# Expert blocks of a decoder layer: where results wait before their scatter, when the sums are loaded, and how the last group is summed

## The chip, the cores and the metric

The kernel runs on one core of a Trainium2 chip. The metric is device time in microseconds; lower is better. A core has a matrix engine (PE; its weight loads are listed as PEld), a vector engine (DVE), a scalar engine (ACT), a general engine (POOL) that also issues the scatters by row number, and a queue engine (SP) that issues most other transfers. The 16 DMA engines carry all transfers. Each engine works through its own list of instructions in order.

## The reference

The input is 32 sequences of 128 rows with 128 features, and a context of the same shape. One decoder layer is computed: causal self-attention with 16 heads, a residual and a layernorm; cross-attention to the context, a residual and a layernorm; then a mixture of eight experts of which each row uses two, a residual and a layernorm.

```python
def _moe(x, rw, rb, w1, b1, w2, b2):
    router_weights = softmax(xf @ rw + rb)
    topw, topi = top_k(router_weights, 2)
    topw = softmax(topw)
    h = gelu(einsum('td,edf->etf', xf, w1) + b1)     # D = 128, FF = 512, E = 8
    eo = einsum('etf,efd->etd', h, w2) + b2
    out = einsum('etd,te->td', eo, combine)
x = layernorm(x + attn(x, x, x, ..., causal))
x = layernorm(x + attn(x, ctx, ctx, ...))
x = layernorm(x + moe(x, ...))
```

All is in float32.

## The kernel before

The 32 sequences form eight groups of four. Attention is a schedule of half slots: `half_slot(h)` does half of the scores of one sequence, parts of older ones, and then the calls that a table holds for that half slot (projections, norms, routing, row scatters). The table is filled by `chain` and `book`, which put each step into the half slot that is least booked by estimated costs.

The experts work on blocks of 128 rows. Each row of x2, the result after the second layernorm, is scattered to two rows of a DRAM buffer `xs` in the order of the experts (L789). There are two phases of four groups each, each with its own buffers and 39 blocks, so 78 blocks in all, 32 row scatters of the second phase and 78 result scatters. The first phase's blocks start once its rows are placed; the routing and the row scatters of the second phase's last groups run beside them, one half slot after each block.

A block needs its expert's weights (`wd`, 514 KB, five places, so four blocks ahead; L854 or L858 on SP), its rows (`xt`, four blocks in one load, L841) turned by PE (`px`, L870) and copied by DVE (`xT`, L885), the first layer (L893), the gelu on ACT (L898), the second layer (L909), a copy of the result by DVE (`ot`, L914), and a scatter of its 128 rows by POOL to the DRAM buffer `eo` (L916). `ot` has four places: the copy of block i waits until the scatter of block i-4 has landed. PE, DVE, ACT, POOL and SP each take the blocks in the order in which `Pipeline.run` writes them: weights of block i+4, first layer of i, second layer and scatter of i-1, and then `beside`, which holds a half slot of attention's end and one step of each running sum.

The sums: when enough result scatters of a group have been issued (`needed(g)` plus four blocks, planned in `summed`), `combine` loads the residual (`acc`, L982) and the group's results (`gt`, L984, which waits on SP until those scatters have landed), waits four steps, adds the two weighted results (L1001), and normalizes (`finish`, `normalize`: statistics on DVE, a power on POOL at L342, four scalings on ACT at L347, two products with the norm's gain and bias on DVE at L1010 and L1012), then stores (L1014). After the last block the sums that are left run alone.

## Time and profile before

The median of three runs is 653.02 us (649.6 to 657.02).

| | |
|---|---|
| profiled execution, its own time | 657.72 us |
| its span on the core | 655.9 us |
| mean granted TensorE clock | 0.953 |
| PE busy | 583.9 us (89%) |
| DVE busy | 434.5 us (66%) |
| ACT busy | 379.8 us (58%) |
| POOL busy | 368.8 us (56%) |
| moved by DMA over the span | 82.52 MB, 126 GB/s on average |

The shares of busy time are averages over attention and experts, which differ: attention needs little of the DMA engines, the blocks need much of them. A stretch must be read by itself. The chain of waits is followed back from the last instruction; a group of instructions is named by its line, engine, and the tiles it writes and reads. A matmul's end is modelled, so a busy PE is not always one at its peak.

### The profile page before, as it was taken

How to read it: one execution, taken by the hardware profiler on the slowest of the kernel's cores; microseconds unless marked ns; L12 is line 12 of the kernel's file. 1: busy time of each engine (PE TensorE's matmuls, PEld its weight loads, DVE VectorE, ACT ScalarE, POOL GpSimd, SP SyncE). 2: the span in 40 equal slices, each digit the busy share in tenths (PEclk: the TensorE clock that was granted, in tenths of full speed). 3: DMA queues.
4: the chain of work that ended last, by engine and by line, in shares of the span. 5: the costliest groups of instructions: out<-in, count | busy, mean ns of one | idle time of the engine just before them, and what ended most of it. 6: DMA issues, size and time to landing. Idle time of an engine off the chain costs nothing.

```text
span 655.9 us, 22713 instructions
## 1 busy us (share of the span) xinstructions
PE 583.9 (89%) x9247; PEld 496.1 (76%) x9247; DVE 434.5 (66%) x1359; ACT 379.8 (58%) x855; POOL 368.8 (56%) x749
## 2 busy tenths in 40 slices
PE   8999899999999799999999988997898888998970
PEld 6777677887877578877777776776887788898970
DVE  4356556767758867887788778984966644543553
ACT  3255456677676357666666666555674456664652
POOL 3256455544645456628836614743888885654661
PEclk9599979999999899999999998997998989999995
DMA  5114420614010011001001100421887999999962
GB/s 138 27 32 71 96 36 2 213 33 168 3 34 3 1 37 49 3 2 55 14 19 31 39 2 10 151 96 49 278 271 230 356 343 370 362 348 389 345 249 74
DMA packets 48040, 82.52 MB, mean 126 GB/s; under 512 B 7968, under 2 KB 26464, under 8 KB 47936
## 3 DMA queue, kind: packets, MB, share of 16 engines
q1 hardware_dynamic: 42816, 71.57, 33.7%
q0 software_dynamic: 4544, 9.38, 3.9%
q8 instruction: 72, 1.18, 0.8%
q14 instruction: 32, 0.26, 0.1%
q10 hardware_dynamic: 576, 0.13, 0.1%
HBM read 62.15 MB, written 23.10 MB: 130 GB/s over the span
## 4 chain that ended last, share of the span: by engine, by line
PE 62%; DVE 20%; DMA 8%; ACT 4%; issue 3%; POOL 3%; SPq 0%; ACTq 0%; DVEq 0%; POOLq 0%
PE ph L893 8%; PE po L909 7%; PE sc_s L453 6%; PE sc_c L453 6%; PE po_s L539 4%; DMA wd<-wpk 4%; DVE m_c L492 4%; PE st_s L465 4%; PE po_c L539 4%; PE sc_s L447 3%; DVE m_s L492 3%; DMA eo<-ot,to 2%; PE st_s L460 2%; PE st_c L460 2%; PE pk_s L396 1%
## 5 line engine op out<-in xcount | busy, mean ns | idle before, releaser
L898 ACT ACTIVATE h<-ph,wd 128x128 f32<-128x128 f32 x312 | 89.0, 370 | 64.1 <-PE ph L893 28.4
L504 POOL TENSOR_SCALAR_AFFINE_SELECT pr_s<-pr_s 128x1024 f32<-128x1024 f32 x64 | 70.1, 1096 | 82.6 <-ACT pr_s L500 82.2
L492 DVE TENSOR_REDUCE m_s<-sc_s 128x8 f32<-128x1024 f32 x64 | 78.2, 1222 | 55.2 <-PE sc_s L453 53.9
L916 POOL DMA_INDIRECT eo<-ot,to x78 | 77.8, 998 | 52.2 <-DVE acc L1001 12.5
L500 ACT ACTIVATE pr_c<-st_c 128x1024 f32<-128x1024 f32 x64 | 65.5, 1024 | 63.2 <-PE st_c L465 61.0
L500 ACT ACTIVATE pr_s<-st_s 128x1024 f32<-128x1024 f32 x64 | 65.5, 1024 | 57.4 <-PE st_s L465 57.2
L893 PE MATMUL ph<-xT,wd 128*128 128x128 f32 x624 | 87.8, 285 | 12.3 <-DMA wd<-wpk 5.5
L492 DVE TENSOR_REDUCE m_c<-sc_c 128x8 f32<-128x1024 f32 x64 | 78.0, 1218 | 24.3 <-PE sc_c L453 16.6
L893 PEld LDWEIGHTS ph<-xT,wd 128*128 128x128 f32 x624 | 78.6, 198 | 17.8 <-DMA wd<-wpk 5.7
L909 PE MATMUL po<-wd,h 128*128 128x128 f32 x624 | 84.2, 279 | 2.2 <-ACT h L898 2.2
L453 PE MATMUL sc_c<-k_c,qb_c 32*128 32x128 f32 x1024 | 75.2, 285 | 11.0 <-DVE m_c L492 9.3
L909 PEld LDWEIGHTS po<-wd,h 128*128 128x128 f32 x624 | 77.5, 195 | 2.8 <-ACT h L898 2.8
L453 PE MATMUL sc_s<-k_s,qb_s 32*128 32x128 f32 x1024 | 76.3, 290 | 0.0
L453 PEld LDWEIGHTS sc_c<-k_c,qb_c 32*128 32x128 f32 x1024 | 62.9, 188 | 17.4 <-DVE m_c L492 13.0
L465 PE MATMUL st_s<-qb_s,k_s 32*128 32x128 f32 x1024 | 72.5, 281 | 0.0
L789 POOL DMA_INDIRECT xs<-x,slots x64 | 64.1, 1002 | 13.0 <-issue 12.4
L465 PE MATMUL st_c<-qb_c,k_c 32*128 32x128 f32 x1024 | 70.5, 276 | 0.0
L465 PEld LDWEIGHTS st_s<-qb_s,k_s 32*128 32x128 f32 x1024 | 67.4, 192 | 0.9
L453 PEld LDWEIGHTS sc_s<-k_s,qb_s 32*128 32x128 f32 x1024 | 67.2, 199 | 0.1
L465 PEld LDWEIGHTS st_c<-qb_c,k_c 32*128 32x128 f32 x1024 | 65.9, 188 | 0.2
L914 DVE COPY ot<-po 128x128 f32<-128x128 f32 x78 | 22.5, 290 | 62.3 <-PE po L909 53.3
L447 PE MATMUL sc_s<-causal,quarter 32*128 32x512 bf16 (+3 forms) x512 | 48.5, 309 | 9.0 <-DVE m_s L492 8.5
(249 smaller groups left out, 1203.6 us busy)
## 6 DMA issues: line engine op xcount, KB each, us to landing
wd<-wpk SPq DMA_DIRECT2D x78, 514.0 KB
xs<-blank SPq DMA_DIRECT2D x2, 2600.0 KB
xt<-xs SPq DMA_DIRECT2D x20, 260.0 KB
wpk<-in_L_xattn_e_w_dram SPq DMA_DIRECT2D x16, 256.0 KB
gt<-eo SPq DMA_DIRECT2D x8, 512.0 KB
xg<-in_x_dram SPq DMA_DIRECT2D x8, 256.0 KB
eg<-in_ctx_dram SPq DMA_DIRECT2D x8, 256.0 KB
x2d<-base SPq DMA_DIRECT2D x8, 256.0 KB
```

What stands on the lines that cost most here:

```text
L447: nc.tensor.matmul(sc[:, i, :, k], lhsT=quarter[rowsof(g), j, :], rhs=bc(causal[rowsof(g), j, k], 1, 4), start=j == 0, stop=False,)
L453: nc.tensor.matmul(sc[:, i, r, :], lhsT=new.group.qb[rowsof(g), r, new.b, :], rhs=new.group.k[rowsof(g), new.b, :], start=not new.masked, ...
L465: nc.tensor.matmul(st[:, i, r, :], lhsT=old.group.k[rowsof(g), old.b, :], rhs=old.group.qb[rowsof(g), r, old.b, :], start=False, stop=r == 3,)
L492: nc.vector.tensor_reduce(new.m[:, 8 * half : 8 * half + 8], sc.rearrange("p i r k -> p (i r) k"), AX.X, ALU.max,)
L500: nc.scalar.activation(old.pr[:, hs, :], st.rearrange("p i r k -> p (i r) k"), AF.Exp, scale=SCALE)
L504: nc.gpsimd.affine_select(out=old.pr[:, hs, :], in_=old.pr[:, hs, :], pattern=[[0, 8], [1, P]], compare_op=ALU.is_ge, fill=0.0, base=0, ch ...
L539: nc.tensor.matmul(po[VC * r : VC * r + VC, g, :], lhsT=u.group.v[:, u.b, at_v : at_v + VC], rhs=u.pr[:, h, :], start=e == 0, stop=e == 1,)
L789: i = nc.gpsimd.indirect_dma_start(out=xs[ph.p][:, :], out_offset=bass.IndirectOffsetOnAxis(ap=slots[:, k, t : t + 1], axis=0), in_=gr.x2[ ...
L893: nc.tensor.matmul(hid[:, c, :], lhsT=w[:, c * P : (c + 1) * P], rhs=self.xT[i // XB][:, i % XB, :], start=True, stop=True,)
L898: nc.scalar.activation(self.h[i][:, c, :], hid[:, c, :], AF.Gelu, bias=w[:, B1 + c : B1 + c + 1])
L909: nc.tensor.matmul(po, lhsT=h[:, c, :], rhs=w[:, W2 + c * P : W2 + (c + 1) * P], start=c == 0, stop=c == NFC - 1,)
L916: s = nc.gpsimd.indirect_dma_start(out=eo[p][:, :], out_offset=bass.IndirectOffsetOnAxis(ap=self.to[q][:, i % XB : i % XB + 1], axis=0), i ...
```

## The change

Results of four blocks share a tile, and there are eleven such tiles, taken in turn from places that attention used (four of `k`, four of `x1`, three of `xT0`). The scatter is a step of its own, `send`: after each block, up to 1.6 scatters a block are issued, less the row scatters that the half slot issued, oldest result first. The target row numbers `to` get ten places instead of three. A sum begins when six more scatters than it needs have been issued (two more for the group before the last), `acc` gets three places, and one more step lies before the store. The x2 of the last two groups is made by DVE instead of POOL. The first rows are fetched and turned a few half slots earlier. The last group is summed in two pairs with operations of their own, and stored by SP and ACT in two transfers.

```diff
+SCATTERS = 1.6
+HELD = ("k",) * 4 + ("x1",) * 4 + ("xT0",) * 3
...
-        nc.gpsimd.tensor_tensor(x2, gr.y, bc(lng[1], 1, G), ALU.mult)
+        engine = nc.vector if gr.gi >= NG - 2 else nc.gpsimd
+        engine.tensor_tensor(x2, gr.y, bc(lng[1], 1, G), ALU.mult)
         yield
-        nc.gpsimd.tensor_tensor(x2, x2, bc(lnb[1], 1, G), ALU.add)
+        engine.tensor_tensor(x2, x2, bc(lnb[1], 1, G), ALU.add)
...
-            self.to[q] = moe.tile([P, XB], U32, tag="to", name=f"to_{p}_{q}", bufs=3)
+            self.to[q] = moe.tile([P, XB], U32, tag="to", name=f"to_{p}_{q}", bufs=10)
...
-            ot = moe.tile([P, P], F32, tag="ot", name=f"ot_{p}_{i}", bufs=4)
-            nc.vector.tensor_copy(ot, po)
+            if q not in self.ot:
+                n = Blocks.held = (Blocks.held + 1) % len(HELD)
+                self.ot[q] = (io if HELD[n] == "xg" else act).tile(
+                    [P, XB, P], F32, tag=HELD[n], name=f"ot_{p}_{q}", bufs=HELD.count(HELD[n])
+                )
+            nc.vector.tensor_copy(self.ot[q][:, i % XB, :], po)
+
+        def send(self, i):
+            q, p = i // XB, self.ph.p
             nc.gpsimd.memset(apart, 0.0)
             s = nc.gpsimd.indirect_dma_start(
...
-                in_=ot, in_offset=None,
+                in_=self.ot[q][:, i % XB, :], in_offset=None,
...
+        def send(self, others):
+            self.may = min(self.may + SCATTERS - others, 2.0)
+            while self.may >= 1.0 and self.ready:
+                k, i = self.ready.pop(0)
+                k.send(i)
+                self.may -= 1.0
...
                 if before:
                     before[0].second_layer(before[1])
+                    self.ready.append(before)
...
+    def last_sums(gr, gt):
+        rs = [small.tile([P, 2, 2], F32, tag="rs", name=f"rs_l{ab.start}") for ab in PAIRS]
+        for n, ab in enumerate(PAIRS):
...
+            for b in range(2):
+                y, t = gr.acc[:, ab.start + b, :], G * gr.gi + ab.start + b
+                for k in range(2):
+                    nc.vector.scalar_tensor_tensor(
+                        y, gt[:, ab.start + b, P * k : P * k + P], wts[:, k, t : t + 1], y,
+                        ALU.mult, ALU.add,
+                    )
+                nc.vector.bn_stats(st[:, b, :], y)
...
+            (nc.sync, nc.scalar)[n].dma_start(
+                out=out[G * gr.gi + ab.start : G * gr.gi + ab.stop].rearrange("b p d -> p b d"),
+                in_=y,
+            )
...
-        gr.acc = moe.tile([P, G, P], F32, tag="acc", name=f"acc_{gr.gi}")
+        gr.acc = moe.tile([P, G, P], F32, tag="acc", name=f"acc_{gr.gi}", bufs=3)
...
-        for _ in range(4):
+        if gr.gi == NG - 1:
+            yield
+            last_sums(gr, gt)
+            return
+        for _ in range(3 if gr.gi == NG - 2 else 4):
             yield
...
-    at(start - 1, blocks.first_rows)
+    at(start - 5, blocks.first_rows)
+    at(start - 2, blocks.turn)
...
-                i = needed(g) + 4
-                key = (p, i) if i < NBL[p] or p == NP - 1 else (p + 1, i - NBL[p])
-                summed[key] = groups["c", g0 + g]
+        def begin_sums():
+            while unsummed:
+                p, g = unsummed[0]
+                if len(phases[p].done) < min(needed(g) + (2 if p == NP - 1 and g == n_last - 2 else 6), NBL[p]):
+                    break
+                sums.append(combine(groups["c", PHASES[p][0] + g]))
+                unsummed.pop(0)
...
         def beside(ph, i):
+            rows = sum(len(phase.sent) for phase in phases)
...
+            blocks.send(sum(len(phase.sent) for phase in phases) - rows)
+            begin_sums()
             step()
+            if ph.p == NP - 1 and i >= NBL[-1] - 3:
+                step()
...
-        sums.extend(combine(gr) for _, gr in sorted(summed.items()))
+        begin_sums()
+        last = sums.pop()
+        next(last)
+        while sums:
+            step()
+        sums.append(last)
         while sums:
             step()
```

## Prediction

> **What bounds the kernel now.** I read the busy time by stretches first, cut where the work changes: expert blocks beside the end of attention (448 to 522 us), beside the last row scatters (to 545), blocks alone (to 635), and the tail. Columns: stretch, length, busy us (and instructions) of PE, PEld, DVE, ACT and POOL, granted TensorE clock, DMA share, GB/s.
>
> ```profile
> 448.00:522.00 74.00, 66.20 (x540) 60.16 (x541) 48.03 (x231) 42.03 (x130) 55.88 (x103) 0.93 0.76 254
> 522.00:545.00 23.00, 20.82 (x171) 20.44 (x170) 10.44 (x45) 12.54 (x44) 17.85 (x34) 0.93 0.98 332
> 545.00:635.00 90.00, 83.47 (x723) 81.33 (x721) 43.83 (x180) 55.45 (x191) 53.40 (x97) 1.00 0.97 355
> 635.00:656.00 21.00, 0.04 (x1) 0.00 (x0) 9.68 (x40) 3.29 (x8) 4.57 (x7) 0.59 0.26 82
> ```
>
> The copies of block results (L914) count the blocks: 25 by 522.4 us, 9 more by 544.9, 44 more by 635.4. That is 2.8 us a block at first (24 steps from 455.3 to 522.1), then 2.5, then 2.06. Only from 522 us on are the DMA engines full. POOL's timeline tells what holds the first stretch:
>
> ```profile
> 480.75 0.96 POOL L789 DMA_INDIRECT xs<-x,slots  x1 [0.21 <-issue]
> 481.71 0.09 POOL L915 MEMSET apart<- 1x1 f32 x1
> 482.02 0.97 POOL L916 DMA_INDIRECT eo<-ot,to  x1 [0.21 <-DVE xT L885]
> 482.98 0.09 POOL L787 MEMSET apart<- 1x1 f32 x1
> 483.29 0.96 POOL L789 DMA_INDIRECT xs<-x,slots  x1 [0.23 <-issue]
> ```
>
> A scatter every 1.27 us, back to back, one of rows and one of results for each block: 2.54 us a block, and POOL does the additions of x2 besides. With four result tiles, a late scatter stops DVE's copy and then PE. The chain of work that ended last says so, next to the second suspect, the weights:
>
> ```profile
> 482.02 7.59 DMA eo<-ot,to
> ...
> 509.36 7.55 DMA wd<-wpk
> ...
> 538.35 6.16 DMA eo<-ot,to
> ```
>
> In the last view the same stretch shows DVE and POOL in each other's way (DVE's and POOL's timelines):
>
> ```profile
> 463.52 1.98 DVE L761 TENSOR_TENSOR slots<-si,ri 128x8 uint32<-128x8 uint32 x1
> ...
> 468.20 1.88 DVE L775 TENSOR_TENSOR sums<-sums,part 128x31 f32<-128x31 f32 x1
> ```
> ```profile
> 464.19 1.28 POOL L608 TENSOR_TENSOR x<-y_c,lng 128x512 f32<-128x512 f32 x1
> ...
> 468.82 1.20 POOL L610 TENSOR_TENSOR x<-x,lnb 128x512 f32<-128x512 f32 x1
> ```
>
> Two tiny DVE operations, 0.17 and 0.19 us in the next round of the same group code, end just when POOL's addition ends.
>
> **Part 1: results wait (HELD, SCATTERS).** The result scatters leave second_layer. Each block may now send 1.6 scatters, the row scatters counting first, and results lie in eleven tiles of four blocks. POOL's share falls from 2.54 to at most 1.6 x 1.27 = 2.03 us a block, and 1.27 is no longer anyone's wait: 44 places against a backlog of some 10 blocks (32 blocks x 0.4, less what gaps give back). The reused tiles (keys, residuals, cross inputs) were last read by attention; only the last residual is still read early in this stretch, by DVE itself, and it is the eighth tile taken. So no new wait at the copies. The row numbers of the targets (to, ten places) are overwritten 40 blocks later: nothing. Nothing is saved in bytes or in POOL's count: 78 + 32 scatters remain, 110 x 1.27 = 140 us, started near 449, plus 8 x 1.35 of normalizations: done by 600, ahead of the end.
>
> What bounds the first 25 blocks then? PE work: a block is 0.89 + 0.89 us in the chain, 25 x 1.78 = 44.5; seven px of 0.44 = 3.1; what is left of attention and routing (po_c, pl, py, ty, to, pu, three pb of 1.05, pw, counts) about 13: 60.6 us at full clock, 65 at the 0.93 granted in this stretch. I take 65, against the 74 of now. DMA would need 0.76 x 74 = 56 us less the deferred loads and scatters, so PE decides here.
>
> **Part 2: earlier start.** px and the first xT move ahead of two small DVE steps and a few PE ones. PE idled 3.29 us on that xT at 448.32 (the profile's idle before L893). I take 2.5 of it: block 25 done at 445.8 + 65 = 511 instead of 522.4, 11 us early. Bounds: 0 and 3.3.
>
> **Part 3: x2 of the last two groups on DVE.** DVE gains four operations of the size of L1010 (0.69 us): 2.8. It loses four stalls: 1.8 and 1.7 above, 0.6 and 1.55 at 489.9 and 492.6, together 5.6; POOL loses 4.95 us. The Trainium skill (SBUF — State Buffer, "Who interferes with whom") says that a DVE instruction with two SBUF inputs and a GpSimd instruction that reads SBUF shut each other out for a whole instruction. That explains the stalls, but speaks against the move too: the new DVE additions could hold POOL's scatters 0.69 each, 2.8 us. By the row it is less: the scatter beside the 0.68 us addition at 634.39 took 1.16 instead of 0.97. I take 0.2 each; POOL has that room now. A new wait comes with the move: DVE, with the result copies queued behind it, now waits until the row scatters of three groups earlier have left the tile. Group 4's last one is issued at 467.8 us and, even at 7.6 us of landing, is through by 475.4; group 7's addition comes near 485. Nothing, then, or 2 us if that scatter comes late. The net 2.8 us of DVE is cover for the 65 of part 1 (PE waited 5.0 us for comb, L621), not added again.
>
> **Part 4: later loads, three acc tiles.** Loads of sums move some seven to nine blocks back; the same bytes. SP's queue holds the weights behind each gt. gt now waits until six more scatters than needed are issued, 7.6 us of POOL, as long as the slowest landing shown (7.59); four blocks of weights lie ahead as cover. I put it at nothing; uncovered, 4 us a load.
>
> **Then the DMA engines.** The stretches need 56.2 + 22.5 + 87.3 = 166 us of full DMA to the end of PE. After block 25 at 511 us, 52 of them are spent (ten scatters, gt and acc of the first group are put off, 1.4 of 18.8 MB). Group 6's loads lie behind the last weights as before, 0.77 MB or 2.1 us. 166 - 52 - 2.1 = 112 us at share 1.0: PE ends at 623. At the 0.97 of the third stretch, 626.5; PE alone would need 53 x 1.89 = 100, so DMA stays the bound, and 11 us won early shrink to 9 or 12. I take 623, 12 early.
>
> **Part 5: the end.** Last group by pairs: from gt's landing at 643.09 to the issue of the output after 652.43 took 9.3 us. In pairs: 3.5 us of sums and statistics, 1.6 POOL, 0.25, 1.0 ACT, 0.75 DVE, 7.1: 2.2 saved. But the order changes: group 5's four normalizations (1.65 us, ACT) now stand ahead of the last block's gelu, and DVE does group 6's sums and statistics (2.3 + 0.7 + 0.7 + 0.9 + 0.35 us) ahead of the last two result copies; the last scatter waits behind POOL's 1.35 us for group 6 too. That puts the last copy 3.5 to 4.5 us later and its scatter some 5. Less concurrent traffic may give 0 to 1.5 back at gt's load (4.36 us now). Net 2.5 later, bounds -1 to 4.
>
> **Sum.** Span 655.9 - 12 + 2.5 = 646.4. The profiled run took 657.72, 1.82 over its span: 648.2, a ratio of 0.9855. It was slower than the median of 653.02, so the forecast is 653.02 x 0.9855 = 643.5.
>
> **Rivals.**
> A. DMA is filled, but at 0.97 or less as now, and the early gain shrinks further: PE clock or DVE steps hold the first 25 blocks at 70 (block 25 at 516), PE ends at 631, tail +2.5: span 654.3, 651 as a median. For it: the chain's 7.55 us at wd at 509 us, before the DMA engines were full; against it, that wd sat behind gt, acc and x2d, which move. Chance 0.22.
> B. All goes well: clock 1.0 early (61 us), DMA 1.0, tail -1: PE ends at 619.5, span 639.3, 636.5 as a median. The windows at 1.02 and 1.03 of DMA share speak for it. 0.23.
> C. Slower: SP's queue becomes the bound. If scatters, now sent in a row without the pauses of PE, take 12 us to land instead of 7.6, each gt load stands 4.4 us past its margin with weights behind it, and the cover of four blocks has gone because DMA is full. Six loads x 4.4 = 26 us take the 12 and 14 more: span 672.4, 669 as a median. It makes the kernel slower by 1% from 2.7 us a load (12 + 6.5 - 2.5 of tail, over six), a landing of 10.3 us. Against it: POOL's order puts scatter 15 near 502 us, and SP reaches that gt only after some 30 blocks, past 515. 0.10.
> D. The tiles don't free anything, since the wait only moves to the weights at once: the first stretch stays at 2.8 us, only the start and the tail count: 653. 0.08. Against it: DMA share of 0.76 there.
> The forecast itself: 0.37.
>
> **Chances.** About 1% (6.5 us) is what a measurement can tell from no change: under 646.5 faster, over 659.5 slower. Forecast and B give faster, with a part of A: 0.66; A's rest and D same: 0.23; C and mishaps at the tail: 0.11. The range goes from a bit under B to a bit over D, 634 to 654.
>
> **What would show it.** Part 1: no wait of the result copy on scatters, POOL's pairs broken by runs of one kind, first 25 blocks within 63 to 67 us, DMA share there near 0.85. DMA step: share 0.97 to 1.02 at 2.1 us a block until PE's end at 620 to 627. Part 3: no DVE operation of 1.5 to 2 us after 450. Part 5: the last copy 4 us after its block, gt to output 7 us. Wrong if DMA share falls under 0.9 after 515 us, or SP waits on gt with PE idle.

## The result, and the profile after

The changed kernel takes 649.41 us (median of 20 runs, 644.11 to 657.76), the kernel before 654.39 (20 runs, 649.33 to 659.5). The ratio is 0.992 with an interval of 0.989 to 0.9949: 0.8% faster, inside the 1% that the prediction called no change, and about half of the 9.5 us that it forecast. The profiled execution took 649.54 us, its span is 647.4.

That holds on the chip of the result. On another chip the same kernel took 6% longer than the kernel before; the experiments come to that.

The busy time by stretches, cut as in the prediction (stretch, length, busy us and instructions of PE, PEld, DVE, ACT and POOL, granted TensorE clock, DMA share, GB/s):

```profile
448.00:522.00 74.00, 71.77 (x608) 66.75 (x608) 46.74 (x241) 47.24 (x151) 54.27 (x104) 1.00 0.90 299
522.00:545.00 23.00, 19.73 (x173) 19.17 (x172) 10.79 (x47) 12.78 (x45) 15.41 (x29) 1.00 1.00 369
545.00:635.00 90.00, 72.85 (x602) 71.03 (x601) 46.04 (x189) 49.57 (x167) 52.99 (x95) 0.92 0.88 313
635.00:647.00 12.00, 0.00 (x0) 0.00 (x0) 5.92 (x22) 1.75 (x4) 1.88 (x4) 0.50 0.31 93
```

PE is busy for 71.8 of the first 74 us, where it had 66.2, at a granted clock of 1.00 instead of 0.93. The DMA engines come in at 0.90 there instead of 0.76. The waits of the result copies from 445 us on (engine, what it waited for: us in all, times, longest) no longer name the scatters of results:

```profile
DVE ot L925 <- PE po L916: 64.0, 53, 4.2
...
PE ph L900 <- DMA wd<-wpk: 10.2, 8, 2.4
...
PEld ph L900 <- DMA wd<-wpk: 9.6, 8, 2.7
```

The same waits in the profile of before:

```profile
DVE ot L914 <- DMA eo<-ot,to: 8.8, 5, 2.6
...
PE ph L893 <- DMA wd<-wpk: 5.5, 6, 1.7
```

The copy of results now waits for PE alone. PE's first layer waits 10.2 us for weights instead of 5.5. Four waits make 8.7 us of the 10.2 (PE's timeline), and each of them ends with weights that SP issued right behind a group's residual and results (`acc`, L1050, and `gt`, L1052, at 521, 553, 586 and 604 us):

```profile
530.35 1.13 PE L900 MATMUL ph<-xT,wd 128*128 128x128 f32 x8 [2.00 <-DMA wd<-wpk]
...
561.69 1.26 PE L900 MATMUL ph<-xT,wd 128*128 128x128 f32 x8 [2.42 <-DMA wd<-wpk]
...
594.82 1.16 PE L900 MATMUL ph<-xT,wd 128*128 128x128 f32 x8 [2.34 <-DMA wd<-wpk]
...
612.49 1.16 PE L900 MATMUL ph<-xT,wd 128*128 128x128 f32 x8 [1.89 <-DMA wd<-wpk]
```

The chain of work that ended last says the same: its scatters of 6 to 8 us have gone, and weights stand in their place, among them the one of 594.82:

```profile
522.84 7.38 DMA wd<-wpk
...
585.30 0.49 SPq L1050
...
586.11 0.33 SPq L1052
...
587.27 7.51 DMA wd<-wpk
```

DVE's timeline shows the two tiny operations that took 1.98 and 1.88 us before:

```profile
457.31 0.17 DVE L766 TENSOR_TENSOR slots<-si,ri 128x8 uint32<-128x8 uint32 x1
...
461.78 0.19 DVE L780 TENSOR_TENSOR sums<-sums,part 128x31 f32<-128x31 f32 x1
```

And the timeline of the end:

```profile
629.04 1.04 POOL L346 TENSOR_TENSOR rs_m<-rs_m,mhalf 128x4 f32<-128x4 f32 x1
...
630.32 1.10 POOL L931 DMA_INDIRECT eo<-ot,to  x1 [0.17 <-DVE rs_m L348]
...
632.96 0.32 SPq L1052 DMA_DIRECT2D gt<-eo  x1
...
636.85 0.74 DVE L1015 SCALAR_TENSOR_TENSOR acc<-gt,wts,acc 128x128 f32<-128x128 f32 x2 [3.43 <-DMA gt<-eo]
...
644.52 0.41 ACTq L1040 DMA_DIRECT2D out_dram<-acc  x1
```

The last scatter of results stands in POOL's list behind the power of the sums' statistics (rs_m), and from the landing of gt to the issue of the last output it takes 7.7 us where it took 9.3.

**Where the 8.5 us between the two profiled spans lie.** Up to the last reduction of attention (line m_c) both kernels run the same list, so I count from its end: 434.4 us in the profile of before, 430.8 in that of after. I take these 3.65 us as the spread of an execution and no part of the change (a second profile of before, e_before below, has 431.6). What is left is 4.85 us. The table has this clock for the profiles of this section and the experiments of the first group below; "last weights" is the end of the last weight packet in the DMA records of the traces, MB and GB/s are all bytes moved from block 25 until then.

| us after attention | first layer starts | block 25 copied | last weights | last first layer | last copy | span's end | MB, GB/s |
|---|---|---|---|---|---|---|---|
| before | 13.9 | 87.9 | 196.4 | 198.8 | 200.6 | 221.5 | 38.73, 357 |
| before, again (e_before) | 13.9 | 84.5 | 195.8 | 198.2 | 200.1 | 221.2 | 38.84, 349 |
| after | 12.2 | 77.4 | 188.0 | 192.0 | 197.7 | 216.6 | 39.44, 357 |
| e_onlyhold | 13.9 | 82.2 | 193.6 | 196.0 | 197.8 | 218.3 | 40.21, 361 |
| e_tail | 12.2 | 77.2 | 190.5 | 193.5 | 195.4 | 216.2 | 39.45, 348 |
| e_plain | 12.2 | 74.2 | 186.7 | 190.4 | 196.1 | 214.1 | 39.71, 353 |
| e_ahead6 | 12.2 | 77.7 | 181.5 | 186.0 | 191.7 | 210.8 | 38.60, 372 |
| e_halfw | 12.2 | 76.0 | | 179.1 | 184.8 | 203.9 | |

Block 25 comes 10.5 us earlier, the last weights 8.4, the last first layer 6.8, the last copy 2.9, the end 4.85. The second profile of before (654.54 us) agrees with the first to 0.6 us in everything but block 25, which it has 3.4 us earlier: part of the 10.5 is spread too. The windows from the first layer to block 25 show where that part lies, in before, e_before, after and e_plain (columns as above):

```profile
448.30:522.30 74.00, 66.50 (x542) 60.46 (x543) 47.94 (x232) 42.33 (x131) 55.88 (x102) 0.94 0.76 256
...
445.50:516.10 70.60, 63.30 (x543) 58.03 (x544) 48.08 (x231) 42.36 (x131) 53.88 (x99) 0.98 0.82 267
...
443.00:508.20 65.20, 63.45 (x543) 58.13 (x544) 44.33 (x235) 42.47 (x132) 46.43 (x91) 0.97 0.83 272
...
439.10:501.10 62.00, 61.30 (x543) 56.76 (x544) 43.24 (x235) 42.24 (x132) 33.63 (x65) 1.00 0.87 282
```

PE's busy time times its granted clock is 62.5, 62.0, 61.5 and 61.3 us: the same work, and the two profiles of before differ by 3.2 us of busy time at clocks of 0.94 and 0.98.

### The profile page after: what moved, and what is told of

Its sections match the earlier page's. It is cut to its first block, busy times and chain, and to the rows that moved or that the text cites. A ratio compares the mean times of both kernels' runs of the same rounds, so it can differ in the third digit from the quotient of the medians.

```text
span 647.4 us, 22655 instructions
## 1 busy us (share of the span) xinstructions
PE 580.8 (90%) x9247; PEld 493.6 (76%) x9247; DVE 431.2 (67%) x1366; ACT 380.0 (59%) x855; POOL 364.1 (56%) x747
## 4 chain that ended last, share of the span: by engine, by line
PE 61%; DVE 16%; DMA 10%; ACT 5%; POOL 3%; issue 2%; SPq 1%; POOLq 0%; DVEq 0%; ACTq 0%
DMA wd<-wpk 8%; PE ph L900 8%; PE po L916 7%; PE sc_c L457 6%; PE sc_s L457 5%; DVE m_c L496 4%; PE po_s L543 4%; PE po_c L543 4%; PE st_s L469 4%; DVE m_s L496 3%; PE sc_s L451 3%; PE st_s L464 2%; PE st_c L464 2%; ACT qb_c L411 1%; PE st_c L469 1%
## 5 line engine op out<-in xcount | busy, mean ns | idle before, releaser
L504 ACT ACTIVATE pr_c<-st_c 128x1024 f32<-128x1024 f32 x64 | 65.5, 1024 | 64.7 <-PE st_c L469 62.5
L931 POOL DMA_INDIRECT eo<-ot,to x78 | 77.2, 990 | 41.9 <-DVE ot L925 10.3
L900 PE MATMUL ph<-xT,wd 128*128 128x128 f32 x624 | 87.3, 284 | 13.1 <-DMA wd<-wpk 10.2
L457 PEld LDWEIGHTS sc_c<-k_c,qb_c 32*128 32x128 f32 x1024 | 63.5, 190 | 17.5 <-DVE m_c L496 13.0
L457 PE MATMUL sc_s<-k_s,qb_s 32*128 32x128 f32 x1024 | 74.9, 286 | 0.0
L457 PEld LDWEIGHTS sc_s<-k_s,qb_s 32*128 32x128 f32 x1024 | 65.8, 195 | 0.1
```

What stands on the lines that cost most here:

```text
L457: nc.tensor.matmul(sc[:, i, r, :], lhsT=new.group.qb[rowsof(g), r, new.b, :], rhs=new.group.k[rowsof(g), new.b, :], start=not new.masked, ...
L504: nc.scalar.activation(old.pr[:, hs, :], st.rearrange("p i r k -> p (i r) k"), AF.Exp, scale=SCALE)
L900: nc.tensor.matmul(hid[:, c, :], lhsT=w[:, c * P : (c + 1) * P], rhs=self.xT[i // XB][:, i % XB, :], start=True, stop=True,)
L931: s = nc.gpsimd.indirect_dma_start(out=eo[p][:, :], out_offset=bass.IndirectOffsetOnAxis(ap=self.to[q][:, i % XB : i % XB + 1], axis=0), i ...
```

## The experiments

The ratio in each is against the kernel before on the same chip. The chips fall into two groups by it: where the result and two of the comparisons were taken the kernel before has a median of 654 to 656 us, on three other chips 678 to 687. I call them the first and the second group; they are told apart because the change has another sign on the second.

### On the first group: what the sum is made of

**e_tail.** The order at the end undone: no double steps, and group 6's sums later.

```diff
-            if ph.p == NP - 1 and i >= NBL[-1] - 3:
-                step()
...
-        for _ in range(3 if gr.gi == NG - 2 else 4):
+        for _ in range(6 if gr.gi == NG - 2 else 4):
```

> The changed kernel, with the steps of the last blocks in another order: no double step beside the last three blocks, and group 6 waits six steps before it sums, so that the last two result copies, the last gelu and the last scatter stand ahead of group 6's sums, statistics and power and of group 5's scalings. Nothing is left out. Theory (the new order at the end gives back what the early blocks won): the last copy comes within 0.5 us of PE's end, its scatter 0.4 us later, the last gt load is issued 4 to 5.5 us earlier against PE's end than in the changed kernel, and the span from PE's natural end falls from 23.7 to 18 or 19 us; ratio to before 0.984 to 0.987. Rival (the end is bound by the landing of the last loads, whatever the order): the gt load lands no earlier, ratio 0.992.

650.08 us, ratio 0.9925 (0.9879 to 0.997). The last copy now comes 1.8 us after the last first layer instead of 5.7, and the last gt 2.8 us earlier; but the end is only 0.4 us earlier, and the ratio is that of the rival. Two reasons. The last group's sums now stand on DVE behind group 6's chain (timeline of this run):

```profile
629.88 0.32 SPq L1052 DMA_DIRECT2D gt<-eo  x1
...
631.87 1.04 POOL L346 TENSOR_TENSOR rs_m<-rs_m,mhalf 128x4 f32<-128x4 f32 x1
...
635.55 0.69 DVE L1085 TENSOR_TENSOR acc<-acc,lnb 128x512 f32<-128x512 f32 x1
636.16 0.73 DVE L1015 SCALAR_TENSOR_TENSOR acc<-gt,wts,acc 128x128 f32<-128x128 f32 x2
```

gt is issued at 629.9, the sums start at 636.2 without a wait for it, right behind group 6's last operation. And the last weights of this execution landed 2.5 us later than those of the profile of after, by a list that is the same up to there. From the last first layer to the end it takes 22.7 us, before 22.7, in the changed kernel 24.6: the new order costs 2.0 us, and this run has them back. It does not have the 18 or 19 us that I expected.

**e_onlyhold.** Part 1 alone, put on the kernel before: HELD, SCATTERS, `send`, and nothing of parts 2 to 5.

```diff
-            ot = moe.tile([P, P], F32, tag="ot", name=f"ot_{p}_{i}", bufs=4)
-            nc.vector.tensor_copy(ot, po)
+            nc.vector.tensor_copy(self.ot[q][:, i % XB, :], po)
...
+                    self.ready.append(before)
```

> The kernel before with only the held results, the paced scatters, and sums that begin when four more scatters than needed have been issued; start, x2 on POOL, two acc places and the old end as before. Nothing is left out. Theory (held results carry the early gain): copies never wait for scatters, the first 25 blocks take 6 to 9 us less than in the kernel before, DMA gives back about half, the tail is as before: ratio 0.993 to 0.996. Rival (x2 on DVE and the early turn carry it): the first 25 blocks gain under 3 us, ratio 0.998 to 1.001.

652.69 us, ratio 1.0001 (0.9959 to 1.0044). The first 25 blocks take 68.3 us, against 74.1 and 70.7 in the two profiles of before; the last weights land 2 to 3 us earlier and the trace ends 3 us earlier. Against the first profile more than half of what the blocks win is gone by the end; against the second they win only 2.4 us, and in the ratio nothing can be told. So my 0.993 to 0.996 did not come, the ratio is in the rival's range, and what part 1 is worth alone on these chips is not shown.

**e_halfw.** Half of the weights' bytes: W1 isn't loaded, the first layer takes W2 in its place.

```diff
-                nc.sync.dma_start(out=wd[:, 0, :], in_=wpk[i])
+                nc.sync.dma_start(out=wd[:, 0, W2:], in_=wpk[i, :, W2:])
...
-                hid[:, c, :], lhsT=w[:, c * P : (c + 1) * P],
+                hid[:, c, :], lhsT=w[:, W2 + c * P : W2 + (c + 1) * P],
```

> The changed kernel, loading only the second half of each block's weights (W2 and biases) and using it for both layers: PE, ACT, DVE and POOL do the same work, the weights' traffic halves from 514 to 258 KB a block; the first layer's own weights are left out, so the result is another. Theory (DMA capacity bounds the blocks after the 25th): DMA share falls to 0.6 to 0.7, blocks run at 1.87 to 1.95 us, PE ends near 53 x 1.9 = 101 us after block 25 instead of 116, ratio to before 0.967 to 0.973. Rival (another engine is as near): POOL's 1.27 us a scatter, ACT or DVE hold the blocks at 2.1 us or more, PE ends less than 6 us earlier, ratio 0.983 or above.

638.65 us, ratio 0.9795 (0.9724 to 0.9866). By stretches:

```profile
522.00:545.00 23.00, 20.84 (x185) 20.47 (x184) 13.47 (x61) 13.47 (x48) 18.67 (x35) 1.00 0.84 262
545.00:610.00 65.00, 61.96 (x545) 60.90 (x544) 36.64 (x153) 42.78 (x147) 44.75 (x81) 1.00 0.86 273
```

With the DMA engines at 0.84 to 0.86 PE is busy for 62 of 65 us. The stretch from block 25 to the last first layer falls from 114.5 to 103.1 us, 1.94 a block, and the end from 216.6 to 203.9. So the transfers, not PE, DVE or POOL, hold that stretch. Halving the weights' bytes is worth 11 to 13 us in this profile, the fastest of the four runs, and some 8 us by the ratios (0.9795 against 0.992). The ratio misses my 0.967 to 0.973, and the DMA share fell to 0.87 from block 25 on (at 269 GB/s), not to 0.6 or 0.7.

**e_ahead6.** Six blocks of weights ahead; to make room, xT and acc go to tiles of attention.

```diff
-AHEAD = 4
+AHEAD = 6
...
-            self.xT[q] = moe.tile([P, XB, P], F32, tag="xT", name=f"xT_{p}_{q}")
+            self.xT[q] = act.tile([P, XB, P], F32, tag="kvT", name=f"xT_{p}_{q}", bufs=3)
```

> The changed kernel with seven places for weights instead of five, loads six blocks ahead (room for them is made by putting acc and xT into tiles that attention no longer needs). Nothing is left out. Theory (the DMA engines' capacity is the bound after block 25): only the 1.03 MB of two more blocks move ahead of the first block, 2.9 us at 355 GB/s; PE ends 2 to 3.5 us earlier, DMA share stays at 0.98 to 1.02, ratio to before 0.987 to 0.989. Rival (the waits for weights are latency, loads of sums standing before them in SP's list): a cover of four more microseconds removes most of the waits of 6 to 7.5 us, PE ends 8 us or more earlier, ratio 0.98. Rival (PE, ACT or POOL bound): no change, 0.992.

641.32 us, ratio 0.9792 (0.9717 to 0.9867): faster than both kernels, by 13.8 and by some 8 us. From block 25 to the last first layer 108.3 us, 6.2 less. The table says how: 38.60 MB instead of 39.44, chiefly the two blocks that were loaded sooner, 2.4 us; and 372 GB/s instead of 357, some 4.3 us, at a DMA share of 1.00 and 0.99; less 0.5 us that PE ends later behind its last weights. The other kernels with whole weights have 348 to 361 GB/s on the first group. In the DMA records a weight packet of 4112 bytes took 175 ns on average in that stretch, 181 in the profile of after; why, I can't say. No wait of PE for weights is left, as the rival of latency had it, and the ratio is the rival's; PE ends 6.2 us earlier, between the theory's 2 to 3.5 and the rival's 8. The rows of the next four blocks have taken the weights' place on the chain:

```profile
523.72 7.87 DMA xt<-xs
556.05 7.50 DMA xt<-xs
564.06 9.91 DMA xt<-xs
584.54 7.59 DMA xt<-xs
```

**e_plain.** The results are written by plain transfers from SP, in the order of the blocks; POOL scatters the inputs alone. The rows of the results then lie in another order, so the output is another.

```diff
-            s = nc.gpsimd.indirect_dma_start(
+            row = FREE[p] + P * i if i < 2 * G * PHASES[p][1] else P * i
+            s = nc.sync.dma_start(out=eo[p][row : row + P, :], in_=self.ot[q][:, i % XB, :])
```

> The changed kernel with every result written by a plain load-and-store transfer from SP's queue, to rows in the order of the blocks, instead of POOL's scatter to each token's row; the rows come out in the wrong order, the bytes are the same, and POOL keeps the scatters of the inputs, half of all. On a chip where the kernel before takes 686 us: theory of the scatters, the waits for nothing that the profile shows fall from 118 us to 60 or less and the time to 670 us or less, ratio 0.95 to 0.98; theory that the waiting results or the tiles they stand in are at fault, they stay at 100 us or more and the ratio at 1.04 or above. On a chip where it takes 650 to 660 us: POOL's scatters bound nothing there by my reading, so the first 25 blocks stay at 64 to 66 us and the ratio at 0.99.

648.9 us, ratio 0.9929 (0.9886 to 0.9972). By stretches:

```profile
440.00:502.00 62.00, 61.30 (x546) 56.76 (x545) 42.43 (x229) 42.12 (x132) 32.90 (x63) 1.00 0.89 288
502.00:540.00 38.00, 33.77 (x297) 33.05 (x296) 16.94 (x71) 21.19 (x75) 1.27 (x2) 1.00 1.00 357
540.00:612.00 72.00, 62.53 (x525) 60.59 (x524) 34.95 (x147) 40.49 (x140) 5.06 (x8) 0.98 1.00 351
```

Without the 78 scatters the first 25 blocks take 62.0 us, 3.2 less, with PE busy for 61.3 of 62. From block 25 on nothing is won: 116.1 us, at a DMA share of 1.00 with POOL nearly idle. Of the 3.2 us, 2.2 are PE's busy time, at a clock of 1.00 instead of 0.97, and 1.0 is idle time. The profiled execution (642.74 us) was also the fastest of ten. So at most some 3 us of the first stretch are POOL's in the changed kernel, and whether it is more than the clock of one execution isn't shown; the ratio of 0.993 has nothing of it.

**e_pause.** Three more memory sets on POOL ahead of each scatter, of inputs and results.

```diff
+            for _ in range(3):
+                nc.gpsimd.memset(pause, 0.0)
             s = nc.gpsimd.indirect_dma_start(
```

> The changed kernel with three more small memory sets on POOL (about 0.3 to 0.5 us in all) ahead of every scatter, of inputs and of results, so that scatters come every 1.6 to 1.8 us instead of 1.27. On a chip where the kernel before takes 686 us: theory that scatters without a pause hold up the others, the waits for nothing that the profile shows fall to 80 us or less and the time by 10 us or more, ratio 1.02 or less; theory that each scatter costs the same wherever it stands, no gain or a loss, 1.05 to 1.07. On a chip where it takes 650 to 660 us: POOL becomes the bound of the first 25 blocks, whose scatters (57 of them by then) take 95 to 100 us, ratio 1.00 to 1.02.

691.62 us, ratio 1.0601 (1.049 to 1.0712), and not in the place that I expected. A scatter comes every 1.7 us, yet the first 25 blocks take 65.1 us as without the pause: the results wait, and PE doesn't notice. The bill comes behind: 149.8 us from block 25 to the last first layer. The waits of that run:

```profile
DVE rs_m L349 <- POOL rs_m L347: 50.0, 7, 18.2
ACT acc L352 <- DVE rs_m L349: 43.6, 7, 16.6
```

The statistics of the sums need a power on POOL, which stands in POOL's list behind scatters; DVE waits for it up to 18.2 us, and the copies of results stand behind DVE's wait. In the changed kernel that wait is 8.1 us in five times, 2.4 at most. So the waiting tiles break one coupling of POOL to PE and leave another.

### On the second group: the other sign

Made to tell parts 1 to 3 and the order of the loads apart, four kernels met a chip where the kernel before takes 685 us. Each is the changed kernel with one edit. e_split loads a group's results in two halves, a block apart:

```diff
+        for part in parts:
+            if gr.gi < NG - 1:
+                yield
+            i = nc.sync.dma_start(out=gt[:, part], in_=rows[:, part])
```

e_nohold undoes part 1:

```diff
-            nc.vector.tensor_copy(self.ot[q][:, i % XB, :], po)
+            self.ot[i] = moe.tile([P, P], F32, tag="ot", name=f"ot_{p}_{i}", bufs=4)
+            nc.vector.tensor_copy(self.ot[i], po)
+            self.send(i)
```

e_late undoes part 2, and e_x2pool part 3:

```diff
-    at(start - 5, blocks.first_rows)
-    at(start - 2, blocks.turn)
+    at(start - 1, blocks.first_rows)
```
```diff
-        engine = nc.vector if gr.gi >= NG - 2 else nc.gpsimd
+        engine = nc.gpsimd
```

> The changed kernel with the eo rows of every group but the last loaded in two halves, one block apart, behind the group's x2 rows which come one block earlier still; same bytes, same four blocks of weights ahead, sums in the same places. Theory of capacity (the stretch from block 25 to the end of the first layers is the bytes over what the DMA engines move): it stays at 114.5 us to within 1, and the ratio to the kernel before stays 0.992. Theory of bursts (768 KB of rows stand in one piece ahead of the weights, 2.1 us at 369 GB/s, and four blocks ahead do not cover them): the waits of the first layer for weights fall by a third or more, the stretch becomes 110 to 112 us, and the ratio 0.986 to 0.988.

> The changed kernel without the waiting results: four single tiles for results, the scatter right behind the copy, as before the change; acc takes other tiles so that all fits. Undoes part 1 alone. Theory of the sum: the copies wait for scatters again, the first 25 blocks take 72 to 74 us instead of 65.2, and what follows is set by the DMA engines and gains nothing, so the end comes 7 to 9 us later: 656 to 658 us, ratio 1.002 to 1.005. Theory that part of the gain is given back to the weights (seen in the two profiles: 110.9 us before and 114.5 after from block 25 on): the stretch behind block 25 gets 3 to 4 us shorter, and the end comes 4 to 5 us later, 653 to 655 us, ratio 0.998 to 1.000.

> The changed kernel with the first rows loaded at the half-slot of before and the first quad transposed inside the run, as before. Undoes part 2 alone. Theory of the sum: the first layer starts 1.7 to 2.5 us later and all behind it too: 651 to 652 us, ratio 0.995. Theory that the weights decide: they are loaded as far ahead by then, the 25 first blocks catch up nothing since PE bounds them, but the stretch behind gets as much shorter, because the DMA engines run on: 649.4 us, ratio 0.992.

> The changed kernel with the two wide operations of x2 of the last two groups on POOL again. Undoes part 3 alone. Theory of the prediction (each of them stalls a copy on DVE, 5.6 us in four stalls, against 2.8 us of work moved): operations of 1 to 2 us on DVE are seen again between 450 and 512, the first 25 blocks take 67 to 68 us instead of 65.2, and the end comes 2 to 3 us later, ratio 0.996. Theory that the stalls have cover now (results wait behind scatters, so a late copy holds only PE's pool of four sums): the 25 blocks stay within 1 us of 65.2, the ratio at 0.992 to 0.993, and only the scatters lag by two or three blocks more.

Ratios: e_split 1.054 (1.0477 to 1.0602), e_late 1.0551 (1.0479 to 1.0623), e_x2pool 1.0513 (1.0455 to 1.057), and e_nohold 0.9914 (0.9866 to 0.9963). No theory had a loss of 5% for three quite different edits. What they share, and e_nohold lacks, is the waiting results. So the changed kernel itself was run again, with e_nohold, e_split and a kernel meant as a better one, e_best2: e_ahead6 with the rows loaded a quad earlier, and the last group's sums ahead of group 6's gain and bias.

```diff
-            self.xt[q] = moe.tile([P, XB, XW], F32, tag="xt", name=f"xt_{p}_{q}", bufs=2)
+            self.xt[q] = moe.tile([P, XB, XW], F32, tag="xt", name=f"xt_{p}_{q}", bufs=3)
...
+        next(last)
+        while sums and not hasattr(groups["c", NG - 2], "scaled"):
+            step()
```

> The changed kernel itself, once more. The three variants e_split, e_late and e_x2pool, each the changed kernel but for one part, and all with waiting results, took 1.05 times the kernel before on a chip on which that one took 685 us, and e_nohold, without them, 0.991. Theory that this comes from the chip (waits of ACT, DVE and PE that end late while POOL sends scatters without a pause): on a chip where the kernel before takes 650 to 660 us the ratio is 0.990 to 0.994 again; on one where it takes 685 us it is 1.04 to 1.06. Theory that it comes from the three edits: the ratio is 0.99 on either.

> e_nohold again (the changed kernel with four single tiles for results and the scatter right behind the copy). On a chip where the kernel before takes 650 to 660 us: theory of the sum, the first 25 blocks take 72 to 74 us instead of 65.2 and nothing behind them gains, 656 to 658 us, ratio 1.002 to 1.005; theory that part is given back to the weights, the stretch behind block 25 gets 3 to 4 us shorter, 653 to 655 us, ratio 0.998 to 1.000. On a chip where it takes 685 us: 0.99 again.

> The changed kernel with six blocks of weights ahead instead of four, three tiles for the rows of a quad and their load one quad earlier, xT and acc in tiles that attention has left, and a new order of the end: the last group's loads and sums ahead of the scale and shift of the group before it. e_ahead6 (the first of these alone) gave 0.979, then waiting for the rows (7.5 to 9.9 us at four places). Theory that PE waits for bursts on the DMA queue: the rows no longer end a wait, the stretch behind block 25 falls from 108.3 us to 105 to 107, the end from 31 us (last first layer to the end 24.8) to 2 us less, and the ratio is 0.972 to 0.976. Theory of capacity: the stretch stays at 108 to 109 and only the end gains, 0.977.

> e_split again (the rows of every group but the last loaded in two halves, a block apart). On a chip where the kernel before takes 650 to 660 us: theory of capacity, the stretch behind block 25 stays at 114.5 us to within 1 and the ratio at 0.992; theory of bursts, the waits of the first layer for weights fall by a third or more, the stretch becomes 110 to 112 us, ratio 0.986 to 0.988. On a chip where it takes 685 us it says nothing of either.

The second group again (686.7 us before): e_after 1.0623 (1.0523 to 1.0722), e_nohold_b 1.0135 (1.0045 to 1.0225), e_best2 1.045 (1.0356 to 1.0544), e_split_b 1.0488 (1.0396 to 1.0579). So it is the chip and the change together: on one chip, in one comparison, the kernel with waiting results takes 1.062 times the kernel before and the one without them 1.014. The first stretch of e_after, 112 us for the work of 65:

```profile
448.00:560.00 112.00, 72.87 (x589) 65.80 (x585) 48.11 (x269) 43.76 (x129) 59.19 (x112) 0.79 0.49 157
```

PE is busy for much the same time, 72.9 us, but idles a third of the stretch, and the DMA engines half of it: neither is the bound. The waits name what ended them in two words only, "issue" (nothing that the profile shows) and "remote" (another core or an unknown queue):

```profile
ACT h L905 <- issue: 65.0, 24, 11.0
...
DVE ot L925 <- remote: 35.2, 4, 14.5
```

The timeline shows one such standstill:

```profile
549.35 0.96 POOL L931 DMA_INDIRECT eo<-ot,to  x1 [0.22 <-issue]
549.78 1.14 ACT L905 ACTIVATE h<-ph,wd 128x128 f32<-128x128 f32 x4 [11.00 <-issue]
...
550.20 2.07 PE L916 MATMUL po<-wd,h 128*128 128x128 f32 x8 [2.89 <-ACT h L905]
...
555.68 0.96 POOL L931 DMA_INDIRECT eo<-ot,to  x1 [0.22 <-issue]
559.62 1.50 SPq L865 DMA_DIRECT2D wd<-wpk  x2
559.62 0.59 DVE L925 COPY ot<-po 128x128 f32<-128x128 f32 x2 [14.47 <-remote]
559.65 0.26 ACT L631 COPY wT<-pw 32x128 f32<-32x128 f32 x1 [8.73 <-remote]
```

By its modelled end PE's product is done at 552.3 us. DVE's copy starts at 559.6, and SP and ACT go on in the same moment, 3.0 us after the last of POOL's scatters that had come every 1.27 us since 534. In all I count waits of over 1.5 us of this kind on PE, ACT and DVE from 445 us on: 12.5 us in the profile of after, 112 in e_after, two thirds of them within runs of scatters longer than 5 us (the expectations below have 118, an earlier count). In the three profiles of e_nohold on the second group it is 47, 48 and 56 us, a quarter of them within such runs.

The trace's semaphore events say more than the two words. Of the 112 us, 104 end within 0.12 us of a signal from PE (21 waits of ACT and DVE), and in 12 of the 21 that signal comes 1.1 to 7.4 us behind the modelled end of PE's last matmul; in the profile of after all six such waits end with a signal 0.01 us behind it. So the others wait for PE. Whether PE's matmuls ended late or only their signals came late isn't told, since a matmul's end is modelled.

e_before is a profile of the kernel before, meant for a chip of the second group too; with e_plain and e_pause it met the first.

> The kernel before, profiled again. On a chip where it takes 686 us: theory that scatters in one piece hold up the other engines, the waits of ACT, DVE and PE for nothing that the profile shows are between those of e_nohold (47 us) and those of the changed kernel (118 us), nearer to e_nohold, since here a result's scatter stands behind its own copy; theory that the chip holds up all kernels alike, they are 110 us or more. On a chip where it takes 650 to 660 us: below 20 us, a first 25 blocks of 73 to 75 us.

It took 654.54 us, with 10 us of such waits and 70.7 us for the first 25 blocks (73 to 75 expected), and is the second look at the kernel before in the table above. e_split_c met the second group a third time:

> e_split once more (the rows of every group but the last loaded in two halves, a block apart; same bytes, same four blocks of weights ahead). On a chip where the kernel before takes 650 to 660 us: theory of capacity, the stretch from block 25 to the end of the first layers stays at 114.5 us to within 1 and the ratio at 0.992; theory of bursts, the waits of the first layer for weights fall by a third or more, the stretch becomes 110 to 112 us, ratio 0.986 to 0.988.

706.45 us, ratio 1.0461 (1.0401 to 1.0522), so bursts against capacity was not settled by it. The last two runs were made for either group and met the second:

> e_nohold once more (the changed kernel with four single tiles for results and the scatter right behind the copy: part 1 undone). On a chip where the kernel before takes 650 to 660 us: theory of the sum, the first 25 blocks take 70 to 74 us instead of 65.2, the last weights land as much later, ratio 1.002 to 1.005. Theory that the weights' transfers, not the copies, set the end (last weights 194 us behind attention in two profiles of the kernel before, 191.7 with part 1 alone, 186 to 188 with all parts), so that part 1 gives 2 to 4 us of the 25 blocks' 6 to 8: the last weights land 188 to 190 us behind attention, ratio 0.996 to 0.999. On a chip where it takes 678 to 687 us: 0.99 to 1.015 as in its two other runs.

> e_plain once more (every result written by a plain transfer from SP's queue, to rows in the order of the blocks, instead of POOL's scatter to each token's row; the rows come out in the wrong order). On a chip where the kernel before takes 678 to 687 us: theory of the scatters, the waits for nothing that the profile shows fall from 118 us to 60 or less, ratio 0.95 to 0.98; theory that the waiting results or their tiles are at fault, they stay at 100 us or more, ratio 1.04 or above. On a chip where it takes 650 to 660 us: 0.993 again, last weights 185 us behind attention.

e_nohold_c 1.0045 (1.0002 to 1.0089), e_plain_b 1.0128 (1.0036 to 1.0221). With the 78 result scatters taken from POOL the waits are 55 us, where the changed kernel had 112 on another chip of the group, as the theory of the scatters said, and the ratio is 1.013 instead of 1.062, though not the 0.95 to 0.98 that I wrote down. The stretches of e_plain_b show where the rest lies:

```profile
448.00:542.00 94.00, 75.94 (x549) 68.93 (x549) 45.81 (x247) 44.57 (x134) 34.77 (x66) 0.84 0.60 193
542.00:657.00 115.00, 100.48 (x872) 97.74 (x871) 54.19 (x228) 65.90 (x226) 7.62 (x12) 1.00 1.00 348
```

While POOL still scatters the inputs, up to about 532 us, the 25 blocks take 91.6 us where the first group had 62.0; as soon as it has none left, PE runs at a clock of 1.00 and the DMA engines at a share of 1.00, as on the first group. That could still be the end of attention, which stops at the same time. The kernels with result scatters speak against it: behind the last scatter of inputs, with attention's end over, e_after has 68 us of such waits and 2.6 us a block, with 62 result scatters still to send; e_nohold, on the same chip with 50 of them, each right behind its copy, has 4 and 7 us and 2.2 us a block in two profiles; e_plain_b has 19 us and 2.4 us a block. So the waits go with POOL's scatters, above all with scatters in a run. That the missing pause is the cause is argued and not shown: no kernel with the pause ran on these chips. By what path the scatters would hold up PE's signals isn't shown either, nor what sets these chips apart. The kernel before has no profile there, so its own waits (it loses 30 us) are not shown either.

What stays inconclusive: e_late and e_x2pool were to price parts 2 and 3 alone. On the second group their intervals overlap that of e_after, so they price nothing.

## Why the prediction was right or wrong

**Part 1, results wait: right in its place, and for a partly wrong reason.** No copy waits for scatters, and the first 25 blocks take 65.2 us where I said 65. I had 60.6 us of PE work stretched by a clock of 0.93. The work was 61.5 us at full clock, and the clock over these blocks 0.97, so PE was busy for 63.5 us; 1.7 us of idle time, which I had at nothing, make the 65.2. That the two errors cancel is luck. e_plain, at a clock of 1.00, takes 62.0, near the 61 of rival B. The gain of 9 us against the one profile of before was smaller against the second: 70.7 to 65.2, 5.5 us. On the second group the part costs far more than it saves (1.062 with it, 1.014 without).

**Part 2, the earlier start: 1.7 us of the 2.5 that I took.** Inside my bounds.

**Part 3, x2 on DVE: right as far as it goes.** The DVE operations of 1.5 to 2 us have gone. Of the scatters beside DVE's four operations one took longer, 1.31 us instead of 0.96; that is less in all than the 0.2 us each that I took from the row, and half of the 0.69 that a whole lockout would have cost it. What the part is worth alone wasn't settled.

**Part 4, later loads: right on the wait that I priced, wrong on the cover.** In the profile of after SP waits twice for scatters ahead of a gt, 0.4 us, and 12.4 us at the last group's, which has no weights behind it. Rival C did not occur on the first group. But I had four blocks of weights as cover and put the loads at nothing, and PE waits 8.7 us in four places for weights issued right behind them; in all it waits 4.7 us more for weights than before. With six blocks ahead (e_ahead6) no such wait is left. Whether the order of the loads or only their bytes make these waits wasn't settled: e_split, made for that, never met the first group.

**"Then the DMA engines": this step failed.** I divided 112 us of DMA work behind block 25 by a share of 1.0, where the kernel before had 0.97, and let PE end with the work. The windows from block 25 to the last weights, before and after:

```profile
522.40:630.80 108.40, 99.69 (x851) 97.33 (x851) 52.05 (x219) 63.92 (x221) 68.36 (x125) 0.98 0.99 357
...
508.20:618.80 110.60, 99.79 (x839) 97.47 (x838) 52.81 (x220) 63.19 (x217) 71.61 (x132) 0.97 0.99 357
```

Up to the last weights the share was 0.99 already, and the rate of 357 GB/s is the same before and after: with four blocks of weights ahead there was nothing left to fill (e_ahead6 alone got more). The 0.97 of my third stretch came from its last 4 us, in which the weights are through and PE works off the blocks it has. That end has no place in my sum, and it grew. After the last weights PE is busy without a break, for 4.0 us to the end of the last first layer (before 2.4) and, as before, 1.8 for the second. So the stretch is 110.6 + 4.0 + 1.8 = 116.4 us where I had 112 (what the new order at the end adds to that is part 5). Before it was 108.5 + 2.4 + 1.8 = 112.7 in the first profile, 115.5 in the second: 3.7 or 0.9 us longer now, where I had it 0.7 shorter. 2.0 of the 3.7 are bytes, 0.71 MB more up to the last weights at 357 GB/s: chiefly seven scatters of 64 KB and the first group's gt, which now come later. Those I had counted (166 - 52 instead of 166 - 56), and the work itself was sized well: 109.8 us of full DMA up to the last weights, where I had 112. The last weights came 8.4 us earlier in the profile of after and 5.9 in that of e_tail, where I let PE end 12 us earlier.

**Part 5, the end: right.** 2.5 us predicted, 2.0 measured (24.6 us from the last first layer to the end, before 22.7; e_tail 22.7). The last copy comes 3.9 us later than before (3.5 to 4.5), and gt to the output takes 7.7 us (7.1).

**The sum: a size, not a sign.** -10.5 to block 25 (I had -11.4), +3.7 behind it (-0.7), +2.0 at the end (+2.5), so -4.8 instead of -9.5. I also carried a ratio over from one execution. Its part behind attention was ordinary, 221.5 us against 221.2 in the second, but within it the first stretch was 3.4 us longer, and I counted those as gain. Against the second profile the sum is -7.1, +0.9 and +1.6. The 651 of rival A comes close in time, and its first half is what happened: the DMA engines were filled no better than before and the early gain shrank. Its reason, 70 us for the first 25 blocks, did not come.

**What no rival had** is the chip. On the second group the change costs 6% (e_after, on one chip; kernels close to it 4.5 to 5.5% on two), and nothing in the profile of before, taken on a chip of the first, could show it.

## What to carry to other kernels

Work that is moved ahead in front of a stretch bound by transfers is worth only as much as the last transfer comes sooner. Read the share of that stretch up to its last needed transfer: an average that takes in the end shows room that isn't there. Then add the work that stands behind the last transfer, and count the bytes that a postponed transfer brings along. Postponing scatters frees the engine that waited for them, but the debt stays in the issuing engine's list, and everything else in that list (here the power for the statistics) becomes the next wait. A gain below 1% from packing one engine's issues more densely should be measured on more than one chip: here it was 0.992 on one and 1.06 on another. A longer queue of weights (0.979 on the first group) was worth more than all the rest. Whether six blocks ahead without waiting results would serve both groups was not tried.

## What the runs showed of the hardware that I had not expected

- On one chip of the second group the changed kernel has 112 us of waits, 104 of them ended by signals of PE, which come up to 7.4 us behind the modelled end of its last matmul, and two thirds of them while POOL issues a scatter every 1.27 us; on a chip of the first group the same list of instructions has 12.5 us, with the signals 0.01 us behind that end.
- All DMA engines busy is not one rate: from block 25 to the last weights after and e_plain moved 357 and 353 GB/s at shares of 0.99 and 1.00, e_ahead6 372 at 1.00.
- The granted clock was low where PE stood still, not where it was busiest: 1.00 at 97% busy (first stretch of after), 0.79 at 65% (e_after), 0.50 with PE idle at the end. It doesn't follow from the busy share alone: the window 448 to 522 us has 0.93 at 89% in before and 1.00 at 90% in e_before.
